# Adapter and mixture-of-experts kernel: nine of sixteen token batches turned by DMA instead of TensorE, the copies of x moved later, and the opening order changed

## The chip, the cores and the metric

The kernel runs on one core of a Trainium2 chip. The metric is the device time of one execution in microseconds (us). Engines are named as in the profile: PE is TensorE (PEld its weight loads), DVE is VectorE, ACT is ScalarE, POOL is GpSimd, SP is SyncE, which here only issues DMAs. SPq, ACTq and POOLq are the instruction queues of engines seen as issuers.

## What is computed

x is 16 batches of 256 tokens, 256 wide, in float32. Each batch has a profile id that picks its adapter.

```python
# adapter, one profile per batch
z = relu(x @ down_w[id] + down_b[id])              # 256 -> 128
y = x + z @ up_w[id] + up_b[id]
a = layernorm(y) * ln_g[id] + ln_b[id]
# feed forward on a
p = softmax(a @ gate_w + gate_b)                   # 8 experts
w = top 2 of p, scaled to sum 1
shared = gelu(a @ sh_w1 + sh_b1) @ sh_w2 + sh_b2   # 256 -> 1024 -> 256
moe = sum over the 2 experts e of  w_e * (gelu(a @ ew1[e] + eb1[e]) @ ew2[e] + eb2[e])
out = x + a + shared + moe
```

## The kernel before

**Units of work.** The tokens of a batch are 2 tiles of 128. Every feed-forward product is made of three float16 products (high by high, high by low, low by high), so the normalized tokens, the weights and the hidden layer are each split into a high and a low half. One shared unit is one batch through the shared weights `wsh`: 8 column groups of 6 matmuls (`mm1`, L692), a gelu per group on ACT (L699), a high half (L707 on ACT or L709 on DVE) and a low half (L713 on DVE) per four groups, then 8 groups of 6 matmuls (`mm2`, L728), then an evacuation on DVE (L1405). Routed units are the same over blocks of 256 tokens gathered for one expert.

**Stages.** Batches 0 to 15 go through the adapter (`adapter_pe`, L869 the product z, L886 and L890 the product up with the bias rows `ubw`), the layer norm (`adapter_ln`, L902 to L970, all DVE) and `payload`. `payload` writes the high half (L990, ACT) and the low half (L995, DVE) of the normalized tokens into `payb` (which the profile calls `late`). These have to be transposed into `xlnT`, because the matmuls contract over the width: eight TensorE transposes per batch (L1006) into a PSUM bank, and one ACT copy (L1014) from there into `xlnT`. `xlnT` then feeds the batch's gate (L1025, 12 small matmuls) and its shared unit. `route` (one group per two batches) finds the top two experts and sends each token's row to its expert's slots in DRAM (`xslot`, L1145, an indirect DMA by POOL). Beside that stage the first 12 shared units run. After the last group, 16 + 16 routed units, 5 half units and the last 4 shared units follow; routed results are added into `yacc` in DRAM by indirect DMA (L1309).

**The opening.** Batch 0 is loaded by SP, then the first half of the shared weights (`pE.ld[0]`, W1, 1 MB, L541), batches 1 to 3, the second half (W2), and so on. `x_scales` needs the largest absolute values of the norm's gains and biases (`gb_t`) and of the gate's weights (`gw32`): three reductions on DVE (L466 to L468), a transpose and a small product on PE (L472, L483), and from these the scale `sx`. `Prep.build` turns float32 weights into halves: a sum of squares on ACT (L557), a column sum over partitions on PE (L580), a few scalars on DVE (L587 to L605), the high half on ACT (L640), the low half on DVE (L646). The shared units start when W1's halves are there.

**Order.** The order of every engine is written out by a planner (`Plan.schedule`) that knows a cost and a due value for each step: it takes the step that can start first by its own costs, and the smaller due value where several can. Its costs and due values (`PIPE`, `PACE`, `P_V`, `VE2`, `W_AT`, `TV` and the like) set the order and nothing else: on the chip each engine runs its instructions in that order and waits for semaphores. `land` is the number of bytes by which the planner sizes a DMA. `after` puts a step behind another in the planner's order without a wait. `idle_pe` (L1667) puts matmuls without a use between PE's steps: `FILL` of them per us of gap that the planner sees, up to `FILL_END`. `X_GATE` holds the copies of x to `yacc` (L1481) behind the norm of a batch.

Of the kernel before, what the change touches and what calls it, by code (L numbers as in the profile page):

```python
# [10 lines left out]
F16 = mybir.dt.float16  # L11
BF16 = mybir.dt.bfloat16
I32 = mybir.dt.int32
AF = mybir.ActivationFunctionType
# [5 lines left out]
P = 128  # L20
NB = 16
S = 256
D = 256
# [5 lines left out]
KC = D // P  # L29
# [23 lines left out]
NWA = 4  # L53
NRW = 3
N_WARM = 28
X_FROM = 5
FILL_END, FILL = 45.0, 3.0
HALF_AT = (2, 5, 8, 11, 14)

O_W1 = 0  # L60
# [10 lines left out]
RSQRT_SEED = float(0x5F3759DF)  # L71

LINK = 0.10
PIPE = 260e3


class Plan:
# [20 lines left out]
    def schedule(self):  # L98
# [8 lines left out]
        while todo:  # L107
# [25 lines left out]
            if o["land"]:  # L133
                pipe = max(end + 1.0, pipe) + o["land"] / PIPE
                end = pipe + 1.0
# [11 lines left out]
        return out  # L147
SC_LAT = 5.0
W_AT, X_AT, X_STEP = 178.0, 100.0, 15.0
P_V = (97.82, 130.39)  # L150
PACE = (0.0, 9.19, 26.59, 14.32)
VE2 = 2.15
TV, WV, PU2, VP = 6.46, 29.82, 10.52, 1.15


@with_exitstack
def adapter_moe_kernel(
# [16 lines left out]
    V, ACT, PE, POOL, SP = nc.vector, nc.scalar, nc.tensor, nc.gpsimd, nc.sync  # L174
# [16 lines left out]
    xlnT = const([P, NB, 2, KC, S], F16, "xlnT")  # L191
# [47 lines left out]
    ident = const([P, P], F16, "ident")  # L239
# [8 lines left out]
    gw32 = const([P, KC, E], F32, "gw32")  # L248
# [19 lines left out]
    plan = Plan()  # L268
# [23 lines left out]
    def pt_of(key):  # L292
        return bank[PT_BANKS[plan.slot["pt", key]]]
# [168 lines left out]
    def x_scales(deps):  # L462
        top = plan.op(
            "DVE", 0.3,
            lambda: (
                V.tensor_reduce(amx0[:, 0:1], gb_t[:, 0:16], AX.X, ALU.max, apply_absolute_value=True),  # L466
                V.tensor_reduce(amx0[:, 1:2], gb_t[:, 16:32], AX.X, ALU.max, apply_absolute_value=True),
                V.tensor_reduce(amx0[:, 2:3], gw32, AX.XY, ALU.max, apply_absolute_value=True),  # L468
            ), 1.15, deps,
        )  # L470
        turn = plan.op(
            "PE", 0.3, lambda: PE.transpose(pt_of("mx0")[0:3, 0:P], amx0, ident32), 1.15, [top],  # L472
            acq=[("pt", "mx0")], lat=0.2, after=[up_of[0]],
        )
        o = tiny(
            [
                lambda: V.tensor_reduce(amc[0:3, :], pt_of("mx0")[0:3, 0:P], AX.X, ALU.max),
                lambda: V.tensor_scalar(amd[0:3, :], ident32[0:3, 0:3], amc[0:3, :], None, ALU.mult),
            ], 1.15, [turn], rel=[("pt", "mx0")], first=0.2,
        )  # L480
        spread = plan.op(
            "PE", 0.2,
            lambda: PE.matmul(  # L483
                pt_of("mx1")[:, 0:3], ones32[0:3, :], amd[0:3, :], start=True, stop=True
            ), 1.15, [o], acq=[("pt", "mx1")], lat=0.2,
        )
        o = tiny(
            [
                lambda: V.tensor_copy(amx, pt_of("mx1")[:, 0:3]),
                lambda: V.tensor_scalar(  # L490
                    mx[:, 0:1], amx[:, 0:1], 16.0, amx[:, 1:2], ALU.mult, ALU.add
                ),
                lambda: V.tensor_copy(mx[:, 1:2], amx[:, 2:3]),
                lambda: V.tensor_scalar(mx, mx, 1e-18, None, ALU.max),
                lambda: V.tensor_scalar(mxe, mx.bitcast(I32), EXP_MASK, None, ALU.bitwise_and),
                lambda: V.tensor_scalar(sx.bitcast(I32), mxe, -1.0, S_BITS, ALU.mult, ALU.add),
                lambda: V.tensor_scalar(rx.bitcast(I32), mxe, R_BITS, None, ALU.subtract),
                lambda: V.tensor_tensor(hbound, amx[:, 0:1], amx[:, 1:2], ALU.add),
                lambda: V.scalar_tensor_tensor(
                    hbound, hbound, 4.0 * 256.0, hbound, ALU.mult, ALU.mult  # L500
                ),
            ], 1.15, [spread], rel=[("pt", "mx1")],
        )
        tiny(
            [
                lambda: V.tensor_tensor(rlog, rx[:, 0:1], rx[:, 1:2], ALU.mult),
                lambda: V.tensor_scalar(gw[:, 0], gw32, sx[:, 1:2], None, ALU.mult),
                lambda: V.scalar_tensor_tensor(
                    gw[:, 1], gw32, sx[:, 1:2], gw[:, 0], ALU.mult, ALU.subtract
                ),  # L510
            ], 1.0, [o],
        )
        return o
# [307 lines left out]
    z_of, ln_done, tc_done, lo_of, gate_of, up_of = {}, {}, {}, {}, {}, {}  # L821
# [3 lines left out]

    A0, PA, U0, PU = PACE

# [89 lines left out]
    def adapter_ln(bs, ydone):  # L917
        key = bs[0]
        n = 2 * len(bs)
        T = lambda name: stb[plan.slot["st", key]][name]  # L920
        va = A(bs[-1]) + 1.5
        bn = []
        for i, b in enumerate(bs):
            for t in range(2):
                bn.append(
                    plan.op(
                        "DVE", 0.33,
                        lambda i=i, b=b, t=t: V.bn_stats(T("st")[:, 2 * i + t, :], base[:, 2 * b + t, :]),
                        va, [ydone[i]], acq=[("st", key)] if not bn else (),
# [25 lines left out]
        for i, b in enumerate(bs):  # L955
# [25 lines left out]
                )  # L981
            ln_done[b] = out2[-1]

    def payload(b):
        y = base[:, 2 * b : 2 * b + 2, :]
        hl = lambda: payb[plan.slot["pay", b]]
        vb = A(b) + 2.0
        hi = plan.op(
            "ACT", 0.66,
            lambda: ACT.activation(hl()[:, :, 0:D], y, AF.Copy, scale=sx[:, 0:1]), vb,  # L990
            [ln_done[b], scaled], acq=[("pay", b)], lat=0.05,
        )
        lo = plan.op(
            "DVE", 0.70,
            lambda: V.scalar_tensor_tensor(  # L995
                hl()[:, :, D : 2 * D], y, sx[:, 0:1], hl()[:, :, 0:D], ALU.mult, ALU.subtract
            ), vb, [hi], lat=0.05,
        )
        lo_of[b] = lo

        def turn():
            pt = pt_of(("x", b)).bitcast(F16).rearrange("p (l k s) -> p l k s", l=2, k=KC)
            for l in range(2):
                for t in range(2):
                    for k in range(KC):
                        PE.transpose(  # L1006
                            pt[:, l, k, t * P : (t + 1) * P],
                            hl()[:, t, l * D + k * P : l * D + (k + 1) * P], ident,
                        )

        T = plan.op("PE", 0.46, turn, vb, [lo], acq=[("pt", ("x", b))], lat=0.3)
        tc_done[b] = plan.op(
            "ACT", 0.95,
            lambda: ACT.activation(  # L1014
                xlnT[:, b].rearrange("p l k s -> p (l k s)"), pt_of(("x", b)).bitcast(F16), AF.Copy
            ), vb, [T, z_of[b]], rel=[("pt", ("x", b))], lat=0.05,
        )

        def gate():
            pg = pt_of(("g", b))[:, 0 : 2 * E].rearrange("p (t e) -> p t e", t=2)  # L1020
            for t in range(2):
                tok = slice(t * P, (t + 1) * P)
                seq = [(xl, wl, k) for k in range(KC) for xl, wl in ((0, 0), (0, 1), (1, 0))]
                for i, (xl, wl, k) in enumerate(seq):
                    PE.matmul(  # L1025
                        pg[:, t, :], xlnT[:, b, xl, k, tok], gw[:, wl, k, :],
                        start=i == 0, stop=i == len(seq) - 1,
                    )

        g = plan.op("PE", 0.36, gate, vb, [tc_done[b]], acq=[("pt", ("g", b))], lat=0.25)  # L1030
        gate_of[b] = plan.op(
            "DVE", 0.2,
            lambda: V.scalar_tensor_tensor(
                L[:, 2 * b : 2 * b + 2, :],
                pt_of(("g", b))[:, 0 : 2 * E].rearrange("p (t e) -> p t e", t=2), rlog,
                gateb_b.unsqueeze(1).broadcast_to([P, 2, E]), ALU.mult, ALU.add,
            ), vb, [g, gateb], rel=[("pt", ("g", b))],
        )
# [312 lines left out]

    idsl = plan.op("SP", 0.45, lambda: SP.dma_start(ids_sb, ids), -1.0, land=99)
    gbl = plan.op("ACT", 0.45, lambda: ACT.dma_start(gb_t, lngb), -0.5, land=P * 128)
    gwl = plan.op("ACT", 0.45, lambda: ACT.dma_start(gw32, gate_w), -0.5, land=P * 64)
    hot_first, hot_all = profile_rows()
    load_batch(0, 0.0, [])
    pE = Prep(E, 2.1, after=[gwl], v2=VE2)
    pE.ld = [pE.load(0, 0.25)]
# [57 lines left out]
    def v_of(s):  # L1416
# [15 lines left out]
        land=P * 1024,  # L1432
# [5 lines left out]
    def top2_weights(v):  # L1438
# [36 lines left out]
        after=[pE.ld[1]],  # L1475
    )
    X_GATE = [ln_done[min(NB - 1, X_FROM + i * (NB - X_FROM) // NB)] for i in range(NB)]
    y_init = [
# [15 lines left out]
    last_ln = ln_done[NB - 1]  # L1494
    prep[0] = Prep(0, P_V[0], after=[z_of[3]])
    prep[0].build(bank_of="pa")
    prep[1] = Prep(1, P_V[1], after=[z_of[7]])
    prep[1].build(bank_of="pa")
# [84 lines left out]
    for e in range(E):  # L1583
        if e >= 2:
            if e == 2:
                after = [ln_done[NB - 1]]
                split = ([ln_done[NB - 1]], [ln_done[NB - 1]])
            else:
                a, b = lasts(e - 3)
                a, b = a + prep[e - 3].stored, b + prep[e - 3].stored  # L1590
                split = (a + b[:1], b)
                after = [ev_last[NSTAT * (e - 3)] if e > 3 else scats[-1][-1]]
# [202 lines left out]
```

## Time and profile before

| | |
|---|---|
| median of 3 runs | 617.91 us (617.55, 617.91, 623.44) |
| the profiled execution | 617.56 us |
| its span, first to last instruction | 615.8 us |
| mean granted TensorE clock | 0.989 |
| PE, DVE, ACT, POOL busy | 97%, 65%, 67%, 48% of the span |
| matmuls L692 and L728 on the chain that ended last | 82% of the span |
| TensorE transposes L1006 | 128 matmuls |
| ACT copies L1014 | 16, 1021 ns each (median) |

The difference of 1.8 us between the profiled execution and its span lies outside the first and the last instruction. A share of busy time is a mean over stages with different limits, so the stages are read one by one.

### The profile page before, as it was taken

To read this page: it belongs to the slowest core of one execution; us is meant where nothing else is said; L and a number is where in the kernel's file an instruction comes from. 1 tells how busy PE (TensorE), PEld (TensorE's weight loads), DVE (VectorE), ACT (ScalarE), POOL (GpSimd) and SP (SyncE) were. 2 spreads that over 40 slices of the span, in tenths; PEclk is the share of its full clock that TensorE was granted. 3 is DMA by queue.
4 is the path that set the end of the run, shared out by engine and by line. 5 is a ranking of instruction groups with operands and counts; after the bars stand their busy time and mean duration, and the time that the engine had idled before them with its cause. 6 is when DMAs were issued, how large, how long until landed. Compare 5 with 4: busy or idle time off the path is not lost.

```text
span 615.8 us, 15254 instructions
## 1 busy us (share of the span) xinstructions
PE 598.0 (97%) x5572; PEld 521.2 (85%) x5572; DVE 401.2 (65%) x1003; ACT 411.7 (67%) x629; POOL 294.9 (48%) x339
## 2 busy tenths in 40 slices
PE   4999999999999999999999999999999999999995
PEld 3568788788898888888888888998989889898884
DVE  4898788988979546687677443554555454544492
ACT  3386767688789758889788666666556555655561
POOL 2004777564655337373474555552645726563200
PEclk8799999999999999999999999999999999999998
DMA  7996785883934497999999898759996698933592
GB/s 240 311 260 225 272 256 189 278 277 107 313 150 129 130 227 86 313 228 230 281 288 239 245 232 173 156 79 315 241 279 75 146 279 171 317 54 36 149 330 92
DMA packets 100329, 129.29 MB, mean 210 GB/s; under 512 B 56574, under 2 KB 83862, under 8 KB 92054
## 3 DMA queue, kind: packets, MB, share of 16 engines
q1 hardware_dynamic: 84514, 110.18, 63.4%
q0 software_dynamic: 15216, 18.01, 15.9%
q8 instruction: 45, 0.74, 0.5%
q14 instruction: 38, 0.31, 0.2%
q10 hardware_dynamic: 516, 0.06, 0.1%
HBM read 92.41 MB, written 46.58 MB: 226 GB/s over the span
## 4 chain that ended last, share of the span: by engine, by line
PE 90%; DMA 5%; ACT 2%; DVE 1%; issue 1%; SPq 0%; POOLq 0%
PE bank L728 41%; PE bank L692 41%; PE bank L886 3%; PE bank L869 2%; DMA wtab<-mc 1%; DMA gw<-in_gate_w_dram 1%; PE bank L890 1%; PE bank L1006 1%; DMA wq<-wtab,idt 1%; PE bank L1025 1%; DMA idt<-xslot 1%; DMA base<-in_x_dram 1%; ACT h L699 0%; ACT hh L707 0%; PE bank L1667 0%
## 5 line engine op out<-in xcount | busy, mean ns | idle before, releaser
L728 PEld LDWEIGHTS <-hh 128*128 128x128 f16 x2424 | 234.9, 98 | 27.3
L699 ACT ACTIVATE h<-bank,tst 128x256 f32<-128x256 f32 x256 | 138.7, 560 | 106.7 <-PE bank L692 103.3
L728 PE MATMUL bank<-wst,hh 128*128 128x256 f16 x1536 | 207.1, 273 | 0.0
L692 PE MATMUL bank<-late,wst 128*128 128x256 f16 x1536 | 203.5, 273 | 0.1
L692 PEld LDWEIGHTS <-wst 128*128 128x128 f16 x1536 | 150.1, 98 | 17.5 <-issue 0.3
L1309 POOL DMA_INDIRECT yacc<-late,idt x47 | 81.0, 1724 | 98.6 <-DVE late L1558 21.8
L1145 POOL DMA_INDIRECT xslot<-late,sli x64 | 67.5, 1054 | 86.0 <-DVE base L961 48.8
L713 DVE SCALAR_TENSOR_TENSOR hh<-h,tst,hh 128x1024 f16<-128x1024 f32 x64 | 82.2, 1284 | 38.4 <-ACT hh L707 37.2
L692 PE MATMUL bank<-xlnT,wsh 128*128 128x256 f16 x768 | 102.1, 272 | 1.1 <-ACT h L699 1.1
L728 PE MATMUL bank<-wsh,hh 128*128 128x256 f16 x768 | 101.5, 272 | 0.0
L699 ACT ACTIVATE h<-bank,tsh 128x256 f32<-128x256 f32 x128 | 69.7, 560 | 47.3 <-PE bank L692 40.0
L1300 POOL DMA_INDIRECT wq<-wtab,idt x69 | 78.9, 1144 | 40.3 <-DMA idt<-xslot 20.9
L692 PEld LDWEIGHTS <-wsh 128*128 128x128 f16 x768 | 73.7, 98 | 11.5 <-issue 1.6
L1309 POOL DMA_INDIRECT yacc<-zT,idt x22 | 37.7, 1712 | 44.7 <-DVE hh L713 8.5
L707 ACT ACTIVATE hh<-h,tst 128x1024 f16<-128x1024 f32 x44 | 50.5, 1147 | 1.3
L1294 DVE SCALAR_TENSOR_TENSOR late<-bank,tst 128x256 f32<-128x256 f32 x44 | 21.3, 483 | 44.7 <-PE bank L728 43.2
L713 DVE SCALAR_TENSOR_TENSOR hh<-h,tsh,hh 128x1024 f16<-128x1024 f32 x32 | 41.0, 1281 | 4.0 <-ACT hh L707 3.8
L707 ACT ACTIVATE hh<-h,tsh 128x1024 f16<-128x1024 f32 x30 | 34.4, 1146 | 0.6
L709 DVE TENSOR_SCALAR hh<-h,tst 128x1024 f16<-128x1024 f32 x20 | 15.4, 770 | 27.7 <-ACT h L699 25.0
L646 DVE SCALAR_TENSOR_TENSOR wst<-wf,prep,wst 128x1024 f16<-128x1024 f32 x20 | 25.4, 1278 | 0.4 <-ACT wst L640 0.4
L1170 POOL IOTA sb_b<- 128x256 int32 x64 | 22.4, 351 | 2.6
L1405 DVE SCALAR_TENSOR_TENSOR base<-bank,tsh,base 128x256 f32<-128x256 f32 x32 | 15.4, 481 | 12.7 <-PE bank L728 12.6
(228 smaller groups left out, 580.8 us busy)
## 6 DMA issues: line engine op xcount, KB each, us to landing
wst<-scr SPq DMA_DIRECT2D x32, 1024.0 KB
scr<-wst SPq DMA_DIRECT2D x16, 1024.0 KB
wf<-scr SPq DMA_DIRECT2D x10, 1024.0 KB
wf<-in_ew_dram SPq DMA_DIRECT2D x6, 1028.0 KB
wf<-in_ew_dram SPq DMA_DIRECT2D x6, 1024.0 KB
wst<-in_adp_dram SPq DMA_DIRECT2D x16, 256.5 KB
xlnT<-in_xT_dram SPq DMA_DIRECT2D x16, 256.0 KB
base<-in_x_dram SPq DMA_DIRECT2D x16, 256.0 KB
```

What stands on the lines that cost most here:

```text
L646: V.scalar_tensor_tensor(self.w[:, a + 2048 : b + 2048], self.wf[h][:, f], sc[:, 2 * h : 2 * h + 1], self.w[:, a:b], ALU.mult, ALU.subtract,)
L692: mm = PE.matmul(pa[:, 0:n_tok], w1[:, wl, c, k, :], xin[:, xl, k, 0:n_tok], start=i == 0, stop=i == len(seq) - 1,)
L699: ACT.activation(h32[:, c % 4, 0:n_tok], pa[:, 0:n_tok], AF.Gelu_apprx_tanh, bias=tail[:, c : c + 1], scale=tail[:, 8:9],)
L707: ACT.activation(hi, h4, AF.Copy, scale=tail[:, 9:10])
L713: V.scalar_tensor_tensor(hh[:, 1, c, 0:n_tok], h32[:, :, 0:n_tok], tail[:, 9:10], hh[:, 0, c, 0:n_tok], ALU.mult, ALU.subtract,)
L728: PE.matmul(py, hh[:, hl, k, t * P : (t + 1) * P], w2[:, wl, k, :], start=q == 0 and i == 0, stop=q == 3 and i == len(seq) - 1,)
L886: PE.matmul(pt_of(("y", b))[:, t * D : (t + 1) * D], zT()[:, t * P : (t + 1) * P], wa()[:, 256:512], start=True, stop=False,)
L1145: ins = POOL.indirect_dma_start(out=xslot[:, :], out_offset=bass.IndirectOffsetOnAxis(ap=sli[:, c, j : j + 1], axis=0), in_=payb[plan.slot ...
L1170: POOL.iota(sb2_b.bitcast(I32), pattern=[[1, D]], base=0, channel_multiplier=0)
L1294: V.scalar_tensor_tensor(ysb, py, tail[:, 10:11], tail[:, 11 : 11 + D], ALU.mult, ALU.add)
L1300: POOL.indirect_dma_start(out=wq[:, t : t + 1], out_offset=None, in_=wtab[:, :], in_offset=bass.IndirectOffsetOnAxis(ap=idt[:, t, 0:2].bit ...
L1309: ins = POOL.indirect_dma_start(out=yacc[:, :], out_offset=bass.IndirectOffsetOnAxis(ap=idt[:, t, 2:4].bitcast(I32), axis=0), in_=ysb, in_ ...
```

## The change

Batches 6 to 14 (`DMA_T`) are no longer turned by TensorE: SP issues two DMA transposes per batch, each from one tile of `payb` straight into `xlnT`. Both wait for the batch's low half. Batches 0 to 5 and 15 keep the TensorE path, which becomes the function `turn_pe`. The copies of x into `yacc` are gated by batches 9 to 15 instead of 5 to 15. The three reductions of `x_scales` come behind the product up of batch 0 in the order. The gate's weights are loaded by SP as its third DMA, ahead of x of batch 0 and of W1, instead of by ACT. The planner's constants change.

```diff
-X_FROM = 5
-FILL_END, FILL = 45.0, 3.0
+X_FROM = 9
+FILL_END, FILL = 32.0, 3.0
...
-PIPE = 260e3
+PIPE = 280e3
...
-P_V = (97.82, 130.39)
-PACE = (0.0, 9.19, 26.59, 14.32)
-VE2 = 2.15
-TV, WV, PU2, VP = 6.46, 29.82, 10.52, 1.15
+DMA_T = range(6, 15)
+P_V = (126.97, 128.92)
+PACE = (0.0, 8.0, 26.47, 14.94)
+VE2 = 5.67
+TV, WV, PU2, VP = 20.53, 41.69, 10.39, 1.11
...
                 V.tensor_reduce(amx0[:, 2:3], gw32, AX.XY, ALU.max, apply_absolute_value=True),
-            ), 1.15, deps,
+            ), 1.15, deps, after=[up_of[0]],
...
+        def turn():
+            for t in range(2):
+                SP.dma_start_transpose(
+                    out=xlnT[:, b, :, :, t * P : (t + 1) * P].rearrange("p l k s -> p (l k) s"),
+                    in_=hl()[:, t, 0 : 2 * D],
+                )
+
+        if b in DMA_T:
+            tc_done[b] = plan.op("SP", 1.0, turn, vb - 0.5, [lo, z_of[b]], land=2 * P * 1800)
+        else:
+            tc_done[b] = turn_pe(b, hl, vb, lo)
...
-    gwl = plan.op("ACT", 0.45, lambda: ACT.dma_start(gw32, gate_w), -0.5, land=P * 64)
+    gwl = plan.op("SP", 0.45, lambda: SP.dma_start(gw32, gate_w), 0.15, land=P * 128)
```

`turn_pe` holds the lines of the old `turn` and of the ACT copy, unchanged.

More of the change, by code (lines that the diff above doesn't have):

```diff
@@ L982, in adapter_ln, with turn_pe @@
             ln_done[b] = out2[-1]
+    def turn_pe(b, hl, vb, lo):
+        def turn():
+            pt = pt_of(("x", b)).bitcast(F16).rearrange("p (l k s) -> p l k s", l=2, k=KC)
+            for l in range(2):
+                for t in range(2):
+                    for k in range(KC):
+                        PE.transpose(
+                            pt[:, l, k, t * P : (t + 1) * P],
+                            hl()[:, t, l * D + k * P : l * D + (k + 1) * P], ident,
+                        )
+        T = plan.op("PE", 0.46, turn, vb, [lo], acq=[("pt", ("x", b))], lat=0.3)
+        return plan.op(
+            "ACT", 0.95,
+            lambda: ACT.activation(
+                xlnT[:, b].rearrange("p l k s -> p (l k s)"), pt_of(("x", b)).bitcast(F16), AF.Copy
+            ), vb, [T, z_of[b]], rel=[("pt", ("x", b))], lat=0.05,
+        )
     def payload(b):
@@ L1001, in turn @@
         def turn():
[L1002 to L1017, printed above, removed]
+            for t in range(2):
+                SP.dma_start_transpose(
+                    out=xlnT[:, b, :, :, t * P : (t + 1) * P].rearrange("p l k s -> p (l k) s"),
+                    in_=hl()[:, t, 0 : 2 * D],
+                )
+        if b in DMA_T:
+            tc_done[b] = plan.op("SP", 1.0, turn, vb - 0.5, [lo, z_of[b]], land=2 * P * 1800)
+        else:
+            tc_done[b] = turn_pe(b, hl, vb, lo)
         def gate():
```

## The prediction

> **What bounds the kernel now.** I read the page first, then a table by stage, then the waits and the timeline of the first 42 us. Busy shares, the granted clock and the chain of the page:
>
> ```profile
> PE 598.0 (97%) x5572; PEld 521.2 (85%) x5572; DVE 401.2 (65%) x1003; ACT 411.7 (67%) x629; POOL 294.9 (48%) x339
> ...
> PEclk8799999999999999999999999999999999999998
> ...
> PE 90%; DMA 5%; ACT 2%; DVE 1%; issue 1%; SPq 0%; POOLq 0%
> ```
>
> PE is on the chain for 90% of the span, and the clock is full but for the first slices. By stage (each engine's busy us, then clock, DMA share, GB/s):
>
> ```profile
> 0.00:29.00 29.00, 20.59 (x107) 13.14 (x108) 18.22 (x102) 10.25 (x12) 3.65 (x33) 0.82 0.85 272
> 29.00:42.00 13.00, 11.49 (x95) 8.64 (x94) 12.95 (x45) 10.17 (x15) 0.00 (x0) 1.00 0.99 222
> 42.00:181.00 139.00, 139.00 (x1348) 115.97 (x1347) 119.10 (x426) 103.19 (x154) 83.00 (x151) 1.00 0.69 236
> 181.00:190.00 9.00, 7.89 (x72) 6.78 (x70) 8.38 (x35) 8.94 (x13) 7.36 (x13) 1.00 0.52 187
> 201.00:601.00 400.00, 399.92 (x3785) 359.82 (x3784) 229.14 (x362) 266.65 (x422) 196.64 (x137) 1.00 0.87 205
> ```
>
> From 42 us on PE is never idle except 1.11 us between 181 and 190. So two things alone shorten the run: less work on PE, or an earlier begin of the unbroken stretch. Before 29 us PE has no product of the shared units at all. What holds the opening:
>
> ```profile
> PE bank L890 <- DVE ubw L449: 6.3, 1, 6.3
> DVE amx L468 <- DMA gw<-in_gate_w_dram: 6.0, 1, 6.0
> ACT wsh L557 <- DMA wf<-in_ew_dram: 5.6, 1, 5.6
> ```
>
> The timeline ties them: DVE stands at L468 until 11.87 for the gate's weights, which ACT issued at 4.74, after W1 (4.65). Behind L468 on DVE are the seven steps that finish `ubw` (11.95 to 14.65), and behind those PE's up of batch 0:
>
> ```profile
> 11.87 0.17 DVE L468 TENSOR_REDUCE amx<-gw 128x1 f32<-128x16 f32 x1 [6.03 <-DMA gw<-in_gate_w_dram]
> 14.70 0.37 PE L890 MATMUL bank<-ubw,hot 24*128 24x256 bf16 x1 [6.26 <-DVE ubw L449]
> 24.04 0.38 PE L580 MATMUL bank<-prep,ones 128*128 128x2 f32 x2
> 26.38 2.18 ACT L640 ACTIVATE wsh<-wf,prep 128x1024 f16<-128x1024 f32 x2
> ```
>
> W1's squares are ready at 15.24 (L557 from 13.25, 1.91 + 0.18), yet its column sum L580 runs at 24.04: on PE it stands behind L472, L483, z and up of batch 1, all late because of L468. The first L692 begins at 29.2.
>
> **The opening after the change.** In the built order the three reductions follow L449 on DVE. So `ubw` goes on at 5.7 and needs the same 2.7 us: ready at 8.4. Up of batch 0 begins at 7.74 as before and ends at about 9.6, against 16.5. The gate's weights, third on SP and issued at about 1.6, cost SP 0.36 us (the ACT issue's row); they should land by 5, well before the reductions at 8.4. W1 goes out some 0.4 us later and lands at 13.7 (between 13.3, if the queue had room, and 14.3, for 256 pieces of 32 bytes in front). Squares end at 15.8.
> Next on PE is z of batch 1, whose tiles are 512 KB behind W1; at the 320 to 400 GB/s of that stretch that is 1.5 us, so 15.2. Up of batch 1 waits for ACT's L880, which stands behind the squares: 15.8 + 0.5 = 16.3, against 22.36, 6 us earlier. Its 1.7 us put L580 at 18.0, the scalars (24.46 to 26.35 before, 1.9) end at 20.3. ACT now has zT of batch 2 (0.47) and the L1014 of batch 0 in front of L640; z of batch 2 and the turn end at 20.3, the copy at 21.3. L640 then begins at 21.4 against 26.38: 5.0 earlier, and the first L692 at 24.2. W2 does not bind: the windows sum to 6.4 MB moved by 24 us, and what stands in SP's order up to W2 is 5.8 MB. The squares of W2 (33.87 before) come behind two gelus instead of three, at about 28. DVE, 12.95 of 13 us busy there, is the counterweight: the built order has more norm and route steps before the first L713, which costs up to 2 us of the lead. I take **-5.0**, between -6.5 and -3.5.
> A rule bears on this. The 2 us windows give PE a clock of 0.50 from 12 to 20 us, behind the gap of 6.26 us. The Trainium skill (TensorE: Matmul & The Clock Gate, rules for kernel authors) wants no idle gap over about 3 us, else the clock halves. The new gap, from the last small product and its fillers (12.6) to z of batch 1 (15.2), is 2.6 us. By the rule the clock stays full, and z and up of batch 1 save another 1 us (z took 1.84 us at 0.50, 0.86 at 1.00). The row only shows that 6 us is too long, and some of this gap is uncertain, so I leave that out.
> Fillers: 31 become 24 in the built order, nearly all in places where PE waits anyway. **0**; the cover gone is a half clock for a few us, +1 at most.
>
> **The turns by DMA.** PE loses 9 x 8 = 72 transposes. The rows:
>
> ```profile
> L1006 PE MATMUL bank<-ident,late 128*128 128x128 f16 x128 | 9.1, 219 | 0.0
> L1014 ACT ACTIVATE xlnT<-bank 128x1024 f16<-128x1024 f16 x16 | 15.9, 1018 | 8.0 <-PE bank L1006 4.5 <-DMA xlnT<-in_xT_dram 1.8 <-PE bank L728 1.6
> L1287 SPq DMA_TRANSPOSE late<-xslot x69: 1209/1256/6236, 195.3 to 538.2; - x69
> 200.00:204.00 4.00, 4.00 (x39) 3.58 (x38) 3.98 (x5) 3.91 (x7) 0.95 (x1) 1.00 0.24 41
> ```
>
> 219 ns is latency. 128 of them fill 9.1 us (71 ns each); on the chain 16 take 0.89 to 1.00 us, 56 to 62 ns. 72 x 62 ns = **-4.5** (4.0 to 5.1), all on the path, since every turn from batch 6 on lies after 42 us. ACT loses 9 x 1.02 = 9.2 us off the path: worth 0, and eases the 181 to 190 stall by at most 1.1.
> What is added: 18 DMA transposes of 128 x 512 halfwords. None of before reads from SBUF; the nearest row is L1287, the same shape from DRAM: 1.26 us of SP each. From 200 to 208 three of them run with little else at a DMA share of 0.24 and 0.23: 0.235 x 8 / 3 = 0.6 us of all 16 engines. Sum: 23 us of SP's issue time and 11 us of DMA, in a stage with share 0.69 over 139 us, so 43 us free. Neither binds.
> The rule that speaks against it: the Trainium skill (VectorE: DVE Perf Modes, the three transpose paths, and its rules) prices a 128 x 128 turn at 390 ns on TensorE and 1309 ns by DMA, and says to use TensorE wherever a PSUM destination will do, as it did here. Eight per batch: 3.1 against 10.5 us, +7.4 per batch, +66 over nine if each lay on the path. The rows give 0.5 us of PE's time against about 2.5 us of issue plus a landing. I follow the rows, for PE is what is scarce: what counts is whether the gate (L1025), the first reader, waits.
> **The new wait.** A batch's pair waits for the low half (L995); on SP, behind it, are loads of later batches and copies of x, none due within 10 us. On PE the gate waits for the pair, and everything on PE stands behind the gate. From L995 to landed I put 2.5 us of issue and 3.8 us (the median of the indirect DMAs xslot<-late from issue to landing): 6.3, an estimate; 4.8 if the SBUF source issues in half the time; 11 with one slow issue (6.2) and queueing. What the order allows, with each L692 or L728 group of six at 0.66 us: from the matmuls whose low half L713 comes next on DVE behind the batch's L995, to the gate, is 0.7 to 7.9 us, mean 2.8, for batches 6 to 14, plus L713's 1.28; before, that distance was negative for all nine. That is the least, since DVE mostly runs ahead of PE; the most, from the L713 before it, is 15 to 25 us. So most gates find their tokens. I take **+1.5**, between 0 and +7.
>
> **The moves.** Copies of x (4.8 MB) begin behind batch 9's norm rather than 5's. Their first reader is the scatter L1309 at 219: **0** by that; late by more than 20 us they would delay POOL, not PE. Weight preparation of experts 0 to 2 moves back by 26, 19 and 21 us of PE work, still ahead of its unit by over 10; four L640 in a row (4.5 us of ACT) may starve PE as at 181 to 190: 0, up to +2. Groups 5 to 7 are routed earlier, so the first routed block has more time. **0**.
>
> **Sum**: -5.0 - 4.5 + 1.5 = -8.0. Against the profiled 617.56 (span 615.8 + 1.8): **609.5**. The median shown, 617.91, stands 0.35 higher.
>
> **Rivals.**
> *The opening does not move* (0.19): batch 1 and 2 arrive with the DMA queue, which is 0.95 or more busy from 8 us, or DVE is full and returns the lead. For it: the second row of the stage table. Against: 5.8 MB before W2 is behind by 24 us. Then 617.6 - 4.5 + 0.5 = 613.5.
> *DVE becomes the bound* (0.08): 119.1 of 139 us busy now; the same work in 133 us is 0.90. For it: the stretch 29 to 42. Against: preparation of expert 2 leaves the stage, and L713 has slack. 3 to 5 us of PE waits: 613.5.
> *Gates wait for the DMA turns* (0.13), the slower side: landing of a pair at 10 us or more, behind copies of x. From 9.5 / 9 = 1.06 us per gate it is slower than before; at 2 us, 617.6 - 9.5 + 18 = 626. For it: every PE step is in order behind the gate. Against: the distances above.
>
> **Numbers.** Forecast 0.60, its own range 604 to 612.5 (-5.1, -6.5 and the old stall of 1.1 at one end, -3.5 and +3 at the other). With the two middle rivals 0.87; the range 604 to 618 holds most of that. A measurement of this kernel tells about 1%, 6.2 us: faster (under 611.7) 0.68, from the forecast's 0.57 and the tail of the middle ones; within 0.21; slower 0.11.
>
> **What would show it.** Right: L580's first run near 18, first L640 near 21, first L692 near 24; 56 transposes at L991 (new numbering); PE idle in the stage up to the routed units under 2 us; the rest of the run as long as before. Wrong: idle of PEld at the gate with a DMA xlnT<-late as releaser; transposes longer than 1.3 us on SPq; the first L692 still near 29; PE idle beside a full DVE.

## The result, and the profile after

The changed kernel takes 623.46 us (median of 20 executions, 618.37 to 627.28) against 617.82 us (20 executions, 616.70 to 623.44): ratio 1.0079, 95% interval 1.0063 to 1.0094. It is 0.8% **slower**; the forecast was 609.5, with a range of its own from 604 to 612.5, and up to 618 with two of the rivals. The profiled execution is the slowest of the twenty (627.28 us; span 625.4 us, mean clock 0.982, where the twenty go from 0.982 to 0.991), so the waits and clocks read below are those of this one execution.

From here on lines are numbered as in the changed kernel: mm1 is L693, mm2 L729, gelu L700, the column sum L581, the high half of weights L641, squares L558, the TensorE turn L991 with its ACT copy L999, the payload's halves L1010 and L1015, the gate L1039, the DMA turn L1023, the numbers of a payload row L1139 (an iota on POOL), the scatter L1159.

The page of after, its busy shares, clock and chain:

```profile
PE 601.4 (96%) x5493; PEld 519.4 (83%) x5493; DVE 392.1 (63%) x998; ACT 410.2 (66%) x625; POOL 305.7 (49%) x339
...
PEclk9779999999999899999999999999999999999999
...
PE 81%; DMA 8%; POOL 3%; ACT 3%; issue 1%; DVE 1%; SPq 1%; ACTq 0%; POOLq 0%
```

TensorE's share of the chain fell from 90% to 81%; DMA, 5% before, and POOL, which was not on it, now have 11% together. The span is 9.6 us longer than before's: PE's idle time has 6.2 us of that (24.0 against 17.8), and its busy time 3.4 us, although 72 transposes are gone; the mean clock is lower (0.982 against 0.989). The table by stage (each engine's busy us, then clock, DMA share, GB/s) says where:

```profile
0.00:29.00 29.00, 24.21 (x125) 15.03 (x126) 21.32 (x109) 11.45 (x14) 3.65 (x33) 0.88 0.90 297
29.00:42.00 13.00, 11.35 (x83) 7.72 (x80) 12.73 (x55) 12.44 (x19) 0.00 (x0) 0.90 0.95 201
42.00:181.00 139.00, 134.58 (x1242) 110.50 (x1242) 117.49 (x442) 92.01 (x135) 90.30 (x155) 0.97 0.76 230
181.00:190.00 9.00, 9.00 (x85) 8.05 (x84) 6.01 (x15) 7.44 (x14) 6.24 (x7) 1.00 0.99 340
201.00:601.00 400.00, 393.08 (x3703) 352.23 (x3701) 219.06 (x358) 270.33 (x422) 201.11 (x138) 1.00 0.86 198
```

PE was never idle in 42 to 181 before; now it is for 4.42 us. In 201 to 601 it was idle for 0.08; now for 6.92. The timeline of PE names the places (last in a row: idle time before it, and what ended it):

```profile
147.30 0.81 PE L693 MATMUL bank<-xlnT,wsh 128*128 128x256 f16 x6 [1.58 <-ACT h L700]
...
154.40 5.76 PE L693 MATMUL bank<-xlnT,wsh 128*128 128x256 f16 x36 [1.74 <-ACT h L700]
...
206.58 1.43 PE L693 MATMUL bank<-late,wst 128*128 128x256 f16 x6 [4.65 <-DMA late<-xslot]
...
222.75 0.82 PE L693 MATMUL bank<-late,wst 128*128 128x256 f16 x6 [1.90 <-ACT h L700]
```

The one at 147.30 is the scatters' too: ACT, whose gelu PE waits for, had just stood for a scatter to give back a payload buffer.

```profile
146.07 0.72 ACT L1010 ACTIVATE late<-base,sx 128x512 f16<-128x512 f32 x1 [1.72 <-DMA xslot<-late,sli]
```

The largest one stands in front of the first routed block, which began at 200.91 without a wait before. Its rows come out of the scatters, and the waits of POOL between 42 and 215 us show what those stood for (us in total, times, longest):

```profile
POOL late L1139 <- DMA xlnT<-late: 14.5, 3, 6.3
...
POOL late L1139 <- DMA xslot<-late,sli: 8.6, 4, 4.5
```

The first row is new, and a product of the change. One iota writes the numbers of both tiles, so its range spans the second tile's row in `payb`, which the DMA turn reads; POOL has to wait for the turn. No gate waits for a DMA turn: the groups of after have only the ACT copies in front of L1039.

```profile
L1039 PE MATMUL bank<-gw,xlnT 128*128 128x8 f16 x192 | 7.2, 167 | 0.4 <-ACT xlnT L999 0.4
L999 ACT ACTIVATE xlnT<-bank 128x1024 f16<-128x1024 f16 x7 | 7.0, 1019 | 0.4 <-PE bank L991 0.3
...
L991 PE MATMUL bank<-ident,late 128*128 128x128 f16 x56 | 4.3, 226 | 0.0
```

The opening did move, by less than forecast (PE's column sum and first mm1, ACT's first high half):

```profile
19.53 0.59 PE L581 MATMUL bank<-prep,ones 128*128 128x2 f32 x2
23.64 2.17 ACT L641 ACTIVATE wsh<-wf,prep 128x1024 f16<-128x1024 f32 x2
25.86 1.14 PE L693 MATMUL bank<-xlnT,wsh 128*128 128x256 f16 x6
```

L581 ran 4.5 us earlier (24.04 before), and took 0.59 us where it took 0.38: the clock was 0.50 from 16 to 22 us.

### The profile page after: what moved, and what is told of

It reads as the page before. It is cut to its first block, busy times and chain, and to the rows that moved or that the text cites. A ratio compares the mean times of both kernels' runs of the same rounds, so it can differ in the third digit from the quotient of the medians.

```text
span 625.4 us, 15113 instructions
## 1 busy us (share of the span) xinstructions
PE 601.4 (96%) x5493; PEld 519.4 (83%) x5493; DVE 392.1 (63%) x998; ACT 410.2 (66%) x625; POOL 305.7 (49%) x339
## 4 chain that ended last, share of the span: by engine, by line
PE 81%; DMA 8%; POOL 3%; ACT 3%; issue 1%; DVE 1%; SPq 1%; ACTq 0%; POOLq 0%
PE bank L693 38%; PE bank L729 37%; DMA xslot<-late,sli 3%; POOL xslot L1159 3%; PE bank L887 2%; DMA xlnT<-in_xT_dram 2%; DMA xlnT<-in_ew_dram 2%; PE bank L870 1%; PE bank L891 1%; DMA late<-xslot 1%; POOL sb_b L1184 1%; ACT wst L641 1%; DMA base<-in_x_dram 1%; ACT h L700 0%; DMA wst<-in_adp_dram 0%
## 5 line engine op out<-in xcount | busy, mean ns | idle before, releaser
L729 PEld LDWEIGHTS <-hh 128*128 128x128 f16 x2424 | 234.7, 98 | 28.9 <-DVE hh L714 0.9
L693 PE MATMUL bank<-late,wst 128*128 128x256 f16 x1536 | 203.6, 274 | 6.9 <-DMA late<-xslot 4.6
L729 PE MATMUL bank<-wst,hh 128*128 128x256 f16 x1536 | 206.1, 273 | 0.0
L700 ACT ACTIVATE h<-bank,tst 128x256 f32<-128x256 f32 x256 | 138.1, 559 | 98.5 <-PE bank L693 92.5
L693 PEld LDWEIGHTS <-wst 128*128 128x128 f16 x1536 | 150.4, 98 | 25.4 <-issue 7.5
L1314 POOL DMA_INDIRECT wq<-wtab,idt x69 | 80.5, 1167 | 65.6 <-DMA idt<-xslot 32.7
L693 PE MATMUL bank<-xlnT,wsh 128*128 128x256 f16 x768 | 104.3, 277 | 4.5 <-ACT h L700 4.4
L1159 POOL DMA_INDIRECT xslot<-late,sli x64 | 74.7, 1168 | 66.6 <-DVE st L929 47.6
L700 ACT ACTIVATE h<-bank,tsh 128x256 f32<-128x256 f32 x128 | 69.8, 561 | 55.4 <-PE bank L693 52.4
L729 PE MATMUL bank<-wsh,hh 128*128 128x256 f16 x768 | 102.2, 274 | 0.6 <-DVE hh L714 0.6
L693 PEld LDWEIGHTS <-wsh 128*128 128x128 f16 x768 | 75.5, 99 | 15.9 <-issue 5.1
L708 ACT ACTIVATE hh<-h,tst 128x1024 f16<-128x1024 f32 x48 | 55.1, 1148 | 1.4
L708 ACT ACTIVATE hh<-h,tsh 128x1024 f16<-128x1024 f32 x30 | 34.3, 1147 | 0.7
L710 DVE TENSOR_SCALAR hh<-h,tst 128x1024 f16<-128x1024 f32 x16 | 12.8, 800 | 19.6 <-ACT h L700 19.6
L887 PE MATMUL bank<-wst,zT 128*128 128x256 f32 x64 | 23.7, 456 | 0.5 <-ACT zT L881 0.3
```

What stands on the lines that cost most here:

```text
L693: mm = PE.matmul(pa[:, 0:n_tok], w1[:, wl, c, k, :], xin[:, xl, k, 0:n_tok], start=i == 0, stop=i == len(seq) - 1,)
L700: ACT.activation(h32[:, c % 4, 0:n_tok], pa[:, 0:n_tok], AF.Gelu_apprx_tanh, bias=tail[:, c : c + 1], scale=tail[:, 8:9],)
L708: ACT.activation(hi, h4, AF.Copy, scale=tail[:, 9:10])
L729: PE.matmul(py, hh[:, hl, k, t * P : (t + 1) * P], w2[:, wl, k, :], start=q == 0 and i == 0, stop=q == 3 and i == len(seq) - 1,)
L887: PE.matmul(pt_of(("y", b))[:, t * D : (t + 1) * D], zT()[:, t * P : (t + 1) * P], wa()[:, 256:512], start=True, stop=False,)
L1159: ins = POOL.indirect_dma_start(out=xslot[:, :], out_offset=bass.IndirectOffsetOnAxis(ap=sli[:, c, j : j + 1], axis=0), in_=payb[plan.slot ...
```

## The experiments

Each kernel was compared with the kernel before on its own chip, so the ratios are what counts; the chips differ (before had medians of 618.36, 618.66, 621.7 and 622.26 us there). My first theory A: the gains are real, and are eaten by a half clock after the fillers left, by late scatters and by late weight preparation. Rival B: the DMA turns are the whole loss. Rival C: the planner's constants are.

### e1: the changed kernel, all turns on TensorE

```diff
-DMA_T = range(6, 15)
+DMA_T = ()
```

> The changed kernel with all batches turned on TensorE again; its constants, its opening and its late copies of x stay. Theory A (the gains are real, but a half clock from 39 to 47 us, scatters that come late before the first routed block, and late weight preparation eat them): 4.5 us of transposes come back, POOL's wait for xlnT<-late (14.5 us) goes, clock and late preparation stay: 620 to 624. Rival B (the DMA turns are the whole loss): 613, since the opening's gain then stands alone. Rival C (the new constants are the loss): 625 or more, with the 4.5 us on top.

Measured: ratio 0.9936 (0.9903 to 0.9968), 0.6% **faster** than before. Without its DMA turns the rest of the change is a gain, as rival B said. The last two scatters and the first routed block in this kernel's timeline:

```profile
176.17 1.24 POOL L1159 DMA_INDIRECT xslot<-late,sli  x1 [0.16 <-issue]
177.71 0.98 POOL L1159 DMA_INDIRECT xslot<-late,sli  x1 [0.30 <-issue]
...
201.60 0.82 PE L693 MATMUL bank<-late,wst 128*128 128x256 f16 x6
```

The scatters end 18 us earlier than in after (195.71), with the same constants, and PE waits for nothing at the first routed block.

### e2: the kernel before, DMA turns alone

The nine batches turn by DMA; constants, opening and copies of x as before.

> The kernel before with one thing of the change: batches 6 to 14 turned by DMA. Constants, fillers, opening and copies of x as before. Theory A: -4.5 us of transposes, +2 to +4 from POOL's wait for the DMA turns: 615 to 618. Rival B: 621 or more. Rival C: 613 to 614.

Measured: ratio 1.0285 (1.0231 to 1.0339), against A and C. PE waits 11.55 us at the first routed block, which begins at 227.84:

```profile
POOL late L1139 <- DMA xlnT<-late: 42.1, 4, 18.6
...
PE bank L693 <- DMA late<-xslot: 11.5, 1, 11.5
```

### e3: the fillers back

```diff
-FILL_END, FILL = 32.0, 3.0
+FILL_END, FILL = 45.0, 3.0
```

> The changed kernel with FILL_END back at 45: the order of all useful steps is unchanged, only matmuls without a use come in between 32 and 45 us. Theory A: granted clock near 1.00 from 36 to 47 us instead of 0.50, so 3 to 5 us less: 618.5 to 620.5. Rival: the clock falls because PE has nothing ready (ACT full), the fillers run into the same gap and the time stays at 623 to 624.

Measured: ratio 1.0017 (0.9989 to 1.0045), median 624.57. In its profile the clock is 1.00 from 36 to 46 us, where after had 0.50 from 40 to 46. So far, and in its ratio (its 618.5 to 620.5 are 1.001 to 1.004), theory A came true. But e4 has no more fillers there than after and shows 1.00 too, and e1, again without them, has 0.52 from 36 to 42. That the missing fillers set the clock is not supported. The ratio lies below that of after, but on another chip, where after was not run; whether fillers gain something stays open.

### e4: the numbers split by tile

```diff
-            POOL.iota(
-                payb[plan.slot["pay", b]][:, :, 2 * D + o : 2 * D + o + 2].bitcast(I32),
-                pattern=[[step, 2], [0, 1]], base=first, channel_multiplier=cm,
-            )
+            for t in range(2):
+                POOL.iota(
+                    payb[plan.slot["pay", b]][:, t, 2 * D + o : 2 * D + o + 2].bitcast(I32),
+                    pattern=[[0, 1]], base=first + step * t, channel_multiplier=cm,
+                )
```

> The changed kernel with the iota that writes the two token numbers of a payload row split by tile, so that its range no longer spans the second tile's row that the DMA transposes read: POOL then waits no more for them; the order stays, POOL runs twice as many iotas. Theory A: L1139's idle behind xlnT<-late (14.5 us) goes, last scatter 1 to 4 us earlier, 1 to 4 us off the run: 619.5 to 622.5. Rival: the scatters were late for the DMA queue or the route's own steps, POOL waits next for something else: 623 to 624.

Measured: ratio 0.9989 (0.9966 to 1.0012), overlapping that of e3 on the same chip and below both expectations (A's 619.5 to 622.5 are 1.003 to 1.008). The wait of 14.5 us is gone from POOL, the last scatter runs at 191.43 instead of 195.71, and PE still waits at the first routed block:

```profile
202.24 1.44 PE L693 MATMUL bank<-late,wst 128*128 128x256 f16 x6 [4.59 <-DMA late<-xslot]
```

POOL now stands for the slots and for its own scatters instead (L1140 here, behind xslot<-late: 10.6 us). The false wait was a part of the lateness at most: the last scatter still runs 13.7 us later than in e1. Something earlier in the chain is late. The order explains it. Counted in groups of six mm1 or mm2 matmuls before it on PE, the gates of batches 6 to 13 stand at 41, 47, 57, 62, 80, 81, 97, 98 in e1 and at 46, 54, 65, 74, 87, 91, 104, 106 in after; in e2 at 71, 73, 88, 90, 121, 125, 137, 147, where before has 55, 57, 72, 75, 103, 104, 116, 117. The planner sizes a DMA turn as 460 KB in its queue, so it puts the gates later. This is theory A2.

### e5: e2 with the numbers split

> The kernel before with batches 6 to 14 turned by DMA, as in e2, and the numbers' iota split by tile, so that POOL no longer waits for the transposes. The order is that of e2. Theory A2 (the DMA turns cost through the chain low half, gate, rank, scatter, first routed block: once by POOL's wait at the numbers, once because the planner, which books 460 KB and a queue for a pair, places the gates 4 to 23 groups of six matmuls later): the first part goes, the second stays: 622 to 632 on the scale of 642 for e2 and 622 for before (ratio 1.00 to 1.016). Rival B (the traffic of the transposes itself slows the scatters): 638 or more.

Measured: ratio 1.0286 (1.0228 to 1.0344), the same as e2. A2 missed: I had expected at least 10 us from the false wait, and no gain can be measured where the ranks behind the late gates arrive late anyway. The number is rival B's (638 or more is a ratio of 1.026), but its mechanism does not show: POOL's numbers wait 5.0 us for scatters to land, 7.1 in before.

### e6: gates planned early again

e4, and the planner books a DMA turn as 3 us of latency:

```diff
-            tc_done[b] = plan.op("SP", 1.0, turn, vb - 0.5, [lo, z_of[b]], land=2 * P * 1800)
+            tc_done[b] = plan.op("SP", 1.0, turn, vb - 0.5, [lo, z_of[b]], lat=3.0)
```

> The changed kernel with the numbers split (e4) and with the DMA turn booked in the planner as 3 us of latency instead of 460 KB of queue: the gates then stand up to 11 groups of six matmuls earlier in PE's order, near where they stand in e1. Theory A2: ranks and scatters come earlier, the wait of 4.6 us at the first routed block shrinks to 0 to 2 us, some gates begin to wait for their transposes (0 to 2 us in sum): ratio to before 0.990 to 0.996. Rival (the booking was right, a pair needs that long): PE waits at the gates for xlnT<-late by as much as it gains, ratio 1.00 or more.

Measured: ratio 1.0066 (1.0031 to 1.0101). The rival came true. The last scatter moved up to 180.99 and PE does not wait at the first routed block; it waits at the gates (PE itself for 6.0 us, its weight loads for 6.8):

```profile
PEld L1039 <- DMA xlnT<-late: 6.8, 6, 2.5
```

With PE idle for 2 to 3 us, gates included, in each of four stretches of 20 to 40 us between 80 and 180, the first routed block begins at 205.24, barely before after's 206.58, and with fewer matmuls in front of it (below). The cautious booking was about right.

### e7: the opening alone

The kernel before with the two edits of the opening (`gwl` on SP, `after=[up_of[0]]`), and nothing else.

> The kernel before with only the opening of the change: the gate's weights loaded by SP in front of x and W1, and the three reductions behind the product up of batch 0. Turns, constants, fillers and copies of x as before; the order of PE up to the first routed block is that of before. Theory A2: the opening's gain (L581 6 us earlier in e1) reaches the first routed block only if scatters keep up, which they do in this order: -3 to -6 us, ratio 0.990 to 0.995. Rival: DVE or the scatter chain returns it: ratio 0.998 to 1.002.

Measured: 612.15 us against 618.36, ratio **0.9893** (0.9845 to 0.9940). It beats both kernels, and A2's 0.990 to 0.995 by a little. PE's timeline and its waits from 42 to 250 us:

```profile
17.86 0.38 PE L581 MATMUL bank<-prep,ones 128*128 128x2 f32 x2
...
23.13 0.82 PE L693 MATMUL bank<-xlnT,wsh 128*128 128x256 f16 x6
...
PE bank L693 <- ACT h L700: 1.1, 2, 0.9
```

The first mm1 comes 6.2 us earlier than before (29.31), and the first routed block too (194.74 against 200.91): the lead arrives in full, because the scatters moved with it (last one 185.94).

### e8: seven payload buffers

```diff
-NPAY = 6
+NPAY = 7
```

> The changed kernel with the numbers split (e4) and seven payload buffers instead of six. Theory A2: the idle time at 140 to 160 us (3.2 us in e4), where ACT stands at the high half L1010 for a buffer and the gelus behind it, shrinks by 2 to 3 us; the wait at the first routed block stays or grows by as much: ratio 0.996 to 0.999, against 0.9989 of e4. Rival: the stall there is ACT's load by the preparation of expert 0 alone: idle unchanged.

Measured: ratio 1.0026 (0.9992 to 1.0060); idle time in 140 to 160 us is 3.69 us, after 3.17 in e4, and 2.42 of it now stand for DVE. But the wait at the first routed block, which was to stay, is gone: the last scatter runs at 185.04, 6.4 us earlier than in e4. In its place PE waits at 170 for ACT, behind a run of four L641 for an expert's weights, where e4 lost 0.5 us between 160 and 180:

```profile
144.05 0.18 PE L1109 MATMUL bank<-M,ltri 128*128 128x32 f16 x1 [2.42 <-DVE M L1096]
...
168.39 4.27 ACT L641 ACTIVATE wst<-wf,prep 128x1024 f16<-128x1024 f32 x4 [0.53 <-DVE prep L606]
...
174.59 3.57 PE L693 MATMUL bank<-xlnT,wsh 128*128 128x256 f16 x18 [4.57 <-ACT h L700]
```

With a seventh buffer (the planned order moved with it) the scatters come earlier, but PE's wait only went elsewhere: the first routed block begins at 202.10, against 202.24 in e4.

### e9: DMA turns in the order of e7

For batches 6 to 14 the functions of the planned TensorE turn and ACT copy are empty, and the DMA turns are issued where the low half stands; every other step keeps its place. After e6 the theory became A3: the DMA turn's longer latency is the cost, and it is paid either at the gate or, where the gates stand later, behind the scatters.

```diff
-        T = plan.op("PE", 0.46, turn, vb, [lo], ...
+        T = plan.op("PE", 0.46, (lambda: None) if b in DMA_T else turn, vb, [lo], ...
...
-            lambda: V.scalar_tensor_tensor(
-                ...
-            ), vb, [hi], lat=0.05,
+            lambda: (
+                V.scalar_tensor_tensor(...),
+                turn() if b in DMA_T else None,
+            ), vb, [hi], lat=0.05,
```

> The kernel of e7 (before with the new opening; 0.9893) with its planned order kept step by step on every engine: for batches 6 to 14 the eight transposes and the ACT copy are left out where they stood, and SP issues the two DMA transposes right behind the low half L1016; the numbers are split as in e4. So nothing is planned anew. Theory A3 (the DMA turn is some 3 to 4 us later than TensorE's, and is paid at the gate where the order leaves no room for it): 4 us of transposes go, nine gates wait 1 to 2 us each, 9 to 18 us: ratio to before 0.996 to 1.012. Rival (only the planner's displaced order made the turns dear): no waits, ratio 0.983.

Measured: ratio 1.0232 (1.0198 to 1.0265), beyond the upper end of A3 and far from the rival. This is the direct price of the DMA turn in a fixed order. PE's waits from 42 to 250 us, and batch 6 on DVE, SP and PE (here the low half is L1016, the DMA turn L1026):

```profile
PEld L1039 <- DMA xlnT<-late: 17.1, 16, 3.1
...
78.91 0.74 DVE L1016 SCALAR_TENSOR_TENSOR late<-base,sx,late 128x512 f16<-128x512 f32 x1
...
79.78 2.70 SPq L1026 DMA_TRANSPOSE xlnT<-late  x2
...
84.52 0.30 PE L1039 MATMUL bank<-gw,xlnT 128*128 128x8 f16 x6 [1.40 <-DMA xlnT<-late]
86.22 0.32 PE L1039 MATMUL bank<-gw,xlnT 128*128 128x8 f16 x6 [1.39 <-DMA xlnT<-late]
```

The low half ends at 79.65; the second tile can be used at 86.22, 6.6 us later. Over the nine batches, the last tile that a gate waited for came 4.2 to 9.3 us behind the low half. In e7 the same batch takes 4.2 us, 2.0 of it until PE comes to the turn:

```profile
79.16 0.74 DVE L1015 SCALAR_TENSOR_TENSOR late<-base,sx,late 128x512 f16<-128x512 f32 x1
...
81.92 0.61 PE L991 MATMUL bank<-ident,late 128*128 128x128 f16 x8
...
82.57 1.02 ACT L999 ACTIVATE xlnT<-bank 128x1024 f16<-128x1024 f16 x1 [1.60 <-PE bank L991]
...
84.13 0.45 PE L1039 MATMUL bank<-gw,xlnT 128*128 128x8 f16 x12
```

The 17.1 us are waits of the weight loads; PE itself stood 14.2 us for the same transfers. That lies in A3's range of waits, and stands against some 4.5 us of transposes. Outside A3 is the clock, which falls to 0.91 in 80 to 120 and to 0.83 in 140 to 160 us, the stretches with the gaps: some 7 us more, by an estimate from these two figures and their lengths. Together that is most of the 19.4 us by which the first routed block begins later than in e7.

### e10: the same in the order of e1

> The same replacement in the order of e1 (the changed kernel's constants, turns on TensorE; 0.9936): the order of e1 kept, the DMA transposes issued behind the low half, numbers split. Theory A3: -4 us of transposes, +5 to +12 us of waits at gates, ratio to before 0.996 to 1.006. Rival (displaced order alone): 0.987.

Measured: ratio 1.0397 (1.0357 to 1.0437): 21.9 us of waits at the gates (13, longest 5.9; 19.4 for PE itself), with clocks of 0.79 in 80 to 120 and 0.82 to 0.92 in the 20 us stretches up to 180. The sign is that of A3; its waits were too small by about half, and I had left the clock out.

### e11: the copies of x moved in e7

```diff
-X_FROM = 5
+X_FROM = 9
```

> The kernel of e7 with one more part of the change: the copies of x into yacc gated by batches 9 to 15. The planner's queue moves with them, so some steps move too. The prediction's step (copies of x: 0): ratio to before as e7, 0.987 to 0.992. Rival (they land among the last scatters and delay the first routed block): POOL's waits for xslot<-late grow and PE waits 2 us or more at the first routed block: 0.994 or more.

Measured: ratio 0.9946 (0.9920 to 0.9973), overlapping that of e7 from another chip, but outside the 0.987 to 0.992 expected and on the rival's side. The spans differ by 1.8 us (611.8, 610.0), and PE idles 2.81 us in 180 to 200 where e7 has 1.11. POOL's wait for xslot<-late did not grow (7.4 us, 7.7 in e7), so the rival's way is not it. PE does stand for 1.69 us at the first routed block (197.54), but behind ACT's L708; and ACT has its four L641 just before in both kernels (from 189.16 here, 189.84 in e7). What delayed L708, and whether the difference is more than noise, stays open.

### e12: the gate's weights early, the reductions in their old place

```diff
-            ), 1.15, deps, after=[up_of[0]],
+            ), 1.15, deps,
```

> The kernel of e7 with the three reductions L467 to L469 back in front of the seven steps that finish ubw, in DVE's order; the gate's weights still come first on SP. The order of PE, ACT and SP is that of e7. The prediction's step (the load of the gate's weights holds ubw; the weights land by 5 us): DVE no longer stands at L469 for more than 1 us, so the place of the reductions does not matter: ratio to before as e7, 0.985 to 0.994. Rival (the weights still come late, the moved reductions made the gain): up of batch 0 waits for ubw again, ratio 0.995 to 1.0.

Measured: ratio 0.9925 (0.9894 to 0.9955), within the interval of e7. DVE does not stand for the gate's weights:

```profile
7.02 0.16 DVE L469 TENSOR_REDUCE amx<-gw 128x1 f32<-128x16 f32 x1
```

L581 runs at 17.69. The place of the load is enough for the gain; that of the reductions adds nothing measurable to it. The reductions moved with the load left in its old place were not run.

## Why the prediction was wrong, point by point

**The opening, -5.0: right, and hidden.** e7 has L581 at 17.86 (18.0 forecast), the first L641 at 20.20 (21.4) and the first mm1 at 23.13 (24.2); e1, with the changed constants, has 17.44, 20.23 and 22.61. By the ratio it is worth 6.6 us, between 3.7 and 9.6. In after only 3.4 us of it show at the first mm1; the clock of 0.50 from 16 to 22 us took most of the rest. The prediction left the gain of a full clock out, but its 1.7 us for the up of batch 1 is the time at 1.00: in after, at 0.50, that up took 2.95 us (16.58 to 19.53).

**Fillers, 0, at most +1: open.** The half clock of after between 38 and 48 us cost about 3.4 us (an estimate: the lost share of the clock in each 2 us window), but e4 has the same fillers and did not lose it.

**The turns, -4.5: right as work, and not seen in the time.** 56 transposes remain, with 4.3 us of PE where 128 had 9.1.

**The new wait, +1.5: the step that failed.** Its estimate of the latency, 6.3 us from the low half to the landed tile with 4.8 to 11 around it, was good (6.6 for batch 6 of e9, 4.2 to 9.3 over the nine). The question I put to it was not: "what counts is whether the gate (L1025), the first reader, waits". In after no gate waits, and the latency is paid all the same. The room that I had found between a batch's low half and its gate, and counted as free, is where: from the end of the low half to the gate's first matmul it is 8.7 us in after (median of batches 6 to 14), against 4.4 in before and e7, 4.0 in e1, 6.4 in e6 and 13.2 in e2. The latency lies in a chain (low half, turn, gate, rank, slots, scatter, first routed block) that ends in a wait of PE, and an order that keeps PE from waiting at the gates moves the rest of that chain back. The runs, by the start of the slots' last step (L1135) for groups 3 and 7, the last scatter, and the first routed block, in us:

| kernel | slots 3 | slots 7 | last scatter | first routed mm1 | its wait | weight loads' waits at gates for DMA |
|---|---|---|---|---|---|---|
| before | 100.15 | 179.87 | 192.11 | 200.91 | 0 | 0 |
| e7, opening alone | 93.97 | 173.69 | 185.94 | 194.74 | 0 | 0 |
| e1, turns on PE | 89.90 | 163.07 | 177.71 | 201.60 | 0 | 0 |
| after | 102.50 | 165.68 | 195.71 | 206.58 | 4.65 | 0 |
| e4, numbers split | 100.47 | 161.57 | 191.43 | 202.24 | 4.59 | 0 |
| e6, gates early | 97.17 | 167.62 | 180.99 | 205.24 | 0 | 6.8 |
| e9, in e7's order | 97.67 | 193.11 | 205.44 | 214.15 | 0 | 17.1 |

In front of the first routed block stand the same 1122 matmuls of the shared units, but for e1 (6 fewer) and e6 (36 fewer, some 4 us of PE).

**"Groups 5 to 7 are routed earlier, so the first routed block has more time. 0": wrong.** Group 7 was routed 14 us earlier than before, as the order had it, and yet its last scatter came 3.6 us later. POOL takes the groups one after another: in e1 the last two groups' slots are 20.1 us apart and the last scatter follows 14.6 us behind them. In after group 3 came 12.6 us later than in e1, and what POOL then had in front of it was not caught up: its scatters of group 7 begin at 175.46, 9.8 us after the slots, and 30 us pass from slots to last scatter. The prediction has no term for this queue. The last eight scatters were slow besides: 20.3 us from the first to the last, 13.7 in e1, with one wait for an earlier scatter to land beside a DMA share of 1.00 in 185 to 190 (0.56 in before). Whether that traffic made the wait was not tested.

```profile
192.82 0.12 POOL L1139 IOTA late<- 128x2 int32 x1 [4.48 <-DMA xslot<-late,sli]
```

**The moves, 0 to +2: too low.** e1 has all of them and no DMA turn, and its PE is idle for 3.6 us in 42 to 181, where before has none: 0.97 behind ACT's run of four L641, 1.44 behind DVE's L1260, the rest in small pieces. In after the wait behind the run of L641 is 1.74 us; before has such a run too, at 151.18, without a wait. The 2.27 us between 220 and 227 are not the moves'. There L558 stood for weights (xlnT<-in_ew_dram) that SP issues behind six loads of routed rows, and these wait for the scatters: 15 us later in after than in e1, where no such wait exists.

```profile
214.71 0.90 SPq L542 DMA_DIRECT2D xlnT<-in_ew_dram  x2
...
199.47 1.15 SPq L542 DMA_DIRECT2D xlnT<-in_ew_dram  x2
```

**Rivals.** "Gates wait for the DMA turns", at 626, came nearest, in part by luck: it looked for the cost at the gates, where in after there is none. The planner had hidden it; e6 and e9 bring it back to that place. DVE did not become the bound: 117.5 us of 139, less than before. "The opening does not move" did not come true; the DMA queue that it called 0.95 or more busy from 8 us is at 0.88 to 0.98 in before, by windows of 4 us. The lower end of the range, 604, is 604.9 by its own terms. And the signs named for being wrong did not come: no gate waits, and the transposes hold SP's queue for 1.23 us in the median (3.24 at most). They looked at the first reader, as the sum did.

How much the DMA turns cost in the changed kernel: between e1 (0.9936) and, on the same chip, e4 and e3 (0.9989 and 1.0017) lie 0.5 and 0.8%, 3 to 5 us; to after's own ratio, from another chip, 1.4% or 9 us. By either, the step that takes 4.5 us off the bounding engine made the kernel slower. In a fixed order it cost more: 3.4% from e7 to e9 and 4.6% from e1 to e10, 21 and 29 us. How the remaining excess of after over e4 divides between the clock, the split and the chips stays open.

## What to carry to other kernels

Before work is moved off the bounding engine onto a DMA, follow its result to the last reader: in these runs the added latency (6.6 us instead of 4.2 in the batch shown) was paid where the bounding engine met that chain again, and the planned order only chose where. A missing wait at the first reader proves nothing; look at the next engine with a queue of its own (POOL here) and at the time from its last input to its last output. And test the parts of a mixed change alone: one small load put first in a queue was worth about 0.7% alone (e12) and 1.1% with the reductions moved (e7), and was buried under the rest.

## What the runs showed of the hardware

A transpose by DMA out of SBUF, 128 x 512 halfwords, held SP's queue for 1.23 us (median of 18 in after), as long as one out of DRAM (1.26 in before); one pair of after stood there for 8.4 us. In e9 a tile that a gate waited for could be read 1.3 to 3.7 us after its issue ended.

The clock was 0.50 (0.60 at its start in e6) between 16 and 22 us in after, e3, e4, e6, e8 and e10, and 1.00 there in e1, e7, e9, e11 and e12. PE's last gap before it was 2.16 us in after, 1.31 in e3 and 0.88 in e4, against 1.41 in e1 and 1.29 in e7; a single gap does not tell the two apart. The rule I had cited from the Trainium skill (TensorE: Matmul & The Clock Gate, "Why this matters for your kernels"), no idle gap over about 3 us, was kept in all of these, and six of the eleven lost the clock. Nor is each of these a property of its kernel: a trace is one execution, and executions of one kernel differ in mean clock, from 0.982 to 0.991 in after and from 0.982 to 0.996 in e1, where 6 us at 0.50 make 0.005 (an estimate from the span). What decides it these runs do not settle.
